# Turning a stored chunk into image order: TensorE transposes from 16 line loads, or VectorE block transposes from 4 quarter loads

## The chip, the cores and the metric

The kernel runs on one core of a Trainium2 chip. The metric is the device time of one execution in microseconds (us). The profile is one execution recorded by the hardware profiler; its span runs from its first to its last instruction.

## The reference

The input `x` is 1024 images of 16 x 16 pixels with 16 channels, in float32 (image, height h, width w, channel c). Four layers follow one another. Each normalises its input in 8 groups of 2 channels, applies an operation and adds the result to its input:

```python
x = x + _L0_conv_ref(_gn(x), core0, core1, core2)      # a tensor-train matrix over (h, w, c)
x = x + _L1_conv_ref(_gn(x), ..., 1)                   # cellular automaton, one step
x = x + _L2_conv_ref(_gn(x), filters, bias)            # 3 x 3 convolution
x = x + _L3_conv_ref(_gn(x), ..., 1)                   # cellular automaton, one step

# one step of the automaton (layers 1 and 3):
p = jnp.concatenate([xt, y1, y2], axis=1)              # the channels and two depthwise 3 x 3 filters of them
h = jax.nn.relu(p.reshape(B * W * Hh, 48) @ fc0_w.T + fc0_b)   # 128 hidden values
d = (h @ fc1_w.T + fc1_b).reshape(B, C, W, Hh)
mask = (pre & post)                                    # a pixel is alive before and after
x = (xt + d) * mask
```

The change touches none of this arithmetic. It concerns how the result of the last layer, for the first half of the images, comes from the kernel's own layout into that of the output.

## The kernel before, in words

The batch is cut into two chunks of 512 images (`NB`). Inside the layers a chunk lies with 128 pixel-and-channel lines on the partitions and its 512 images along each partition, in 32 such tiles: 64 KB in each partition, 8 MB a chunk. Two buffers of this size, `X0` and `X1`, hold a chunk each; between layers the chunks go through DRAM tensors `xf[layer][chunk]`. In `xf[4][0]`, the last layer's result for the first chunk, the shape is (8, 4, 128, 512): pairs of columns, quarters q of the channels, 128 lines (4 channels, 2 columns v of the pair, 16 heights h), 512 images. An image of the output has h, w and c along the free axis instead, so lines and images have to be exchanged.

The end of the program is what matters here. `layer_nca` (lines 1256 to 1474) is the automaton. It runs as layer 3 for chunk 0, and then for chunk 1. Per chunk it has 64 groups ("quads") of 4 output rows. For a row, TensorE makes the hidden layer in a PSUM bank `ph` by matmuls that use 32 of its 128 rows each, four of them side by side (line 1464); ScalarE applies ReLU into `hid` (line 1467). For a group, TensorE then multiplies four `hid` tiles into a bank `po` (line 1317), two groups to a bank. VectorE adds bias and input to it and frees the bank (`u`, line 1329). GpSimd applies the mask and adds the residual (lines 1366 and 1367). In the first quarter of a chunk VectorE also makes the alive flags and masks (lines 1325, 1347, 1361, 1362), from counts `pcnt` of TensorE (line 1356). The order of the slots is written out by `plan()`.

For chunk 0 a finished tile is stored to `xf[4][0]` (line 1369). For chunk 1 it stays on chip: `turn` inside `layer_nca` (line 1376) transposes it by four matmuls with an identity into a bank `ptx`, and two copies (`evac`, line 159, on VectorE in this part) put it into `xo`, which takes the room of `X0`. At the very end eight DMAs of 1 MB (line 1606) store chunk 1.

`output_steps(0)` (lines 951 to 984) is the work that is woven into chunk 1's automaton: for each height h of chunk 0, `load` brings 256 lines from `xf[4][0]`, `turn` exchanges lines and images, and `store` writes 512 pieces of 1 KB to the output. `run(layer, us, loads, *spans)` places such background steps: a step with a cost is put at a share of the main steps in proportion to the costs before it, a bare function costs 1, a number is a pause, and `(0, f)` costs nothing and comes at the place of what follows it. The order on each engine is the order of the calls; nothing reorders it afterwards. All the DMAs of this part are issued by SP, in order: `xs` loads (line 959), stores from `xo` (line 970), the residual fetches `res` (line 1298), weights `wq` (line 1275) and neighbour lines `nx` (line 1291).

In this part the PSUM banks are 6 for `h` (`ph`, `pcnt`) and 2 for `o`, which `po`, `ptx` and `ptout` take in turn (`shared[0] = "o"`). `xs` and `xo` of `output_steps` have two buffers each.

Of the kernel before, what the change touches and what calls it, by code (L numbers as in the profile page):

```python
# [18 lines left out]
B, S, C = 1024, 16, 16  # L19
P = 128  # L20
NB = 512
# [82 lines left out]
def conv_preact_kernel(ctx: ExitStack, tc: tile.TileContext, a: dict, out: bass.AP):  # L104
    nc = tc.nc
    V, A, G, T = nc.vector, nc.scalar, nc.gpsimd, nc.tensor
# [9 lines left out]
    xf = [  # L116
        [dram.tile([8, 4, P, NB], F32, tag=f"xf{l}_{n}", name=f"xf{l}_{n}") for n in range(NCH)]
        for l in range(5)
    ]
# [16 lines left out]
    def work(shape, tag, name, dt=F32):  # L136
        p, sizes = pool["sb"]
        return p.tile(shape, dt, tag=tag, name=name, bufs=sizes[tag])
# [3 lines left out]
    def bank(shape, tag, name):  # L142
        p, sizes = pool["ps"]
        if tag == "mw":
            either[0] ^= 1
            tag = "mw"[either[0]]
        return p.tile(shape, F32, tag=tag, name=name, bufs=sizes[tag])

    def psum(shape, name):
        return bank(shape, shared[0], name)  # L150
# [3 lines left out]
    def evac(dst, src):  # L154
        flip[0] ^= 1
        if flip[0] and not on_vector[0]:
            A.copy(dst, src)
        else:
            V.tensor_copy(dst, src)


    ident = const.tile([P, P], F32, tag="ident", name="ident")
# [503 lines left out]
    def rstd(st, rows=slice(0, P)):  # L666


        def root():
            st["t"] = work([P, NB], "s", "t")  # L670
            A.activation(st["t"][rows], st["ve"][rows], AF.Sqrt)

        def newton():
            ve, t = st["ve"][rows], st["t"][rows]
            st["r"] = work([P, NB], "n", "r")
            r = st["r"][rows]
            V.reciprocal(r, t)
            V.tensor_tensor(t, r, r, ALU.mult)
            V.tensor_tensor(t, t, ve, ALU.mult)
            V.tensor_scalar(t, t, -0.5, 1.5, ALU.mult, ALU.add)  # L680
            V.tensor_tensor(r, r, t, ALU.mult)

        return [2, root, 3, (6, newton)]
# [64 lines left out]
    def alone(N, q):  # L748

        return (  # L750
            N["sums"][q] + [3, N["mean"][q], 1, N["held"][q], 1] + N["sq"][q]
            + [3, N["var"][q], 1, N["keep"][q]]
        )
# [18 lines left out]
    def scaled(N, qs):  # L772
        steps = [N["spread"][qs[0]], 2, N["held"][qs[0]], 2]
        for q in qs:
            mul = N["mul"][q]
            if q < qs[-1]:
                mul = woven(mul, (2, N["spread"][q + 1]), (3, N["held"][q + 1]))
            steps += mul
        return steps
# [27 lines left out]
    def rows_in(t, w):  # L807

        return t[w // 2].rearrange("q (c v h) b -> v (q c) h b", v=2, h=S)[w % 2]
# [141 lines left out]
    def output_steps(n):  # L951

        steps = []

        def load(h, st):
            st["x"] = work([P, 2, NB], "xs", "xs")
            st["o"] = work([P, 4, 2, P], "xo", "xo")
            for w in range(S):
                nc.sync.dma_start(  # L959
                    st["x"][16 * (w % 8) : 16 * (w % 8) + 16, w // 8], rows_in(xf[4][n], w)[:, h]  # L960
                )

        def turn(bg, st):
            pt = psum([P, 2, P], "ptout")
            for wh in range(2):
                T.transpose(pt[:, wh], st["x"][:, wh, bg * P : bg * P + P], ident)  # L966
            evac(st["o"][:, bg], pt)

        def store(h, st):
            nc.sync.dma_start(  # L970
                out[n * NB : n * NB + NB, h].rearrange("(g b) w c -> b g (w c)", g=4),
                st["o"].rearrange("p g w c -> p g (w c)"),
            )

        sts = [{} for _ in range(S)]
        steps += [lambda: load(0, sts[0]), 4]
        for h in range(S):
            if h + 1 < S:
                steps.append((0, lambda h=h: load(h + 1, sts[h + 1])))
            for bg in range(4):  # L980
                steps.append(lambda h=h, bg=bg: turn(bg, sts[h]))
            steps.append((0, lambda h=h: store(h, sts[h])))
        return steps


# [544 lines left out]
    with ExitStack() as es:  # L1530
# [3 lines left out]
        loads, stat, lines, tail = input_steps(0, tag, 0, nc.sync)  # L1534
# [12 lines left out]
        loads, stat, lines, tail = input_steps(1, tag, 2, G)  # L1547
# [15 lines left out]
        for q in range(4):  # L1563
            bg = alone(N, q - 1) if q else [0.0]
            if q == 3:
                bg = bg + rstd(nst, slice(0, 96)) + [3] + scaled(N, range(3))
# [31 lines left out]
    with ExitStack() as es:  # L1598
        stage(es, dict(nca_sb, xs=2, xo=2), nca_ps)

        xo = X0.rearrange("p n b -> p (n b)").rearrange("p (g h w c) -> p g h w c", g=4, h=S, w=S)
        run(layer_nca(X1, 1, 3, L3, xo), 280, (), (output_steps(0), 0.0, 1.0))
        for h in range(0, S, 8):
            for g in range(4):
                b0 = NB + g * P
                nc.sync.dma_start(
                    out[b0 : b0 + P, h : h + 8].rearrange("b h w c -> b (h w c)"),
                    xo[:, g, h : h + 8].rearrange("p h w c -> p (h w c)"),
                )
# [27 lines left out]
```

## Time and profile before

| what | us |
|---|---|
| median of 3 runs | 3128.32 (3127.24 to 3139.66) |
| the profiled execution's own time | 3130.22 |
| its span | 3128.5 |
| mean granted TensorE clock | 0.981 |
| TensorE matmul busy | 3025.4, 97% of the span |
| VectorE busy | 1747.8, 56% |
| ScalarE busy | 1101.7, 35% |
| GpSimd busy | 685.6, 22% |
| chunk 0's automaton in layer 3, on TensorE | 2528.7 to 2787.6 |
| chunk 1's automaton in layer 3, on TensorE | 2787.6 to 3104.7 |
| last stores, after TensorE's last instruction | 3104.7 to 3128.5 |

The three stretches at the end are read from TensorE's instructions in order of time: the first is between the last convolution matmul and the first automaton matmul of the other chunk, the second ends with the last matmul of all. In the listings, a line of the timeline gives the start in us, the duration, the engine, the line of the kernel, the operation with output and input by the program's names, the shape, and how many instructions were merged into it; what stands in brackets is how long the engine sat idle before it, and what ended that. A float32 matmul leaves two records, so a group of four shows as x8. A few per cent of the matmul records are missing from a trace, so that some counts fall short.

### The profile page before, as it was taken

The numbers are of one execution on the slowest core, as the hardware profiler recorded it, in microseconds if no ns is written. First come the engines' busy times: TensorE is split into PE (matmuls) and PEld (weight loads), VectorE is DVE, ScalarE is ACT, GpSimd is POOL, SyncE is SP. The second block draws the span as 40 slices with busy tenths as digits, with TensorE's granted clock in tenths as the row PEclk, the third lists the DMA queues.
The fourth block names the chain that finished last, engine by engine and source line by source line (L and its number), as shares of the span: only waits on it lengthen the run. The fifth ranks groups of instructions, "written<-read, shape, count | busy, mean of one in ns | idle before, by whom it ended". The sixth has DMA issues, their size and how long they took to land.

```text
span 3128.5 us, 37206 instructions
## 1 busy us (share of the span) xinstructions
PE 3025.4 (97%) x13874; PEld 1261.2 (40%) x13874; DVE 1747.8 (56%) x2330; ACT 1101.7 (35%) x1798; POOL 685.6 (22%) x738
## 2 busy tenths in 40 slices
PE   7999899999999999999999999999989999999996
PEld 5544334444444444444444433333333333333332
DVE  5264237555554555544556678558767748755222
ACT  4431341000000100000111266666665755655553
POOL 1125650200000000000000034435532224432221
PEclk8999999999999999999999999999999999999998
DMA  7644654533334333322222254454455764434445
GB/s 281 237 129 99 141 123 157 174 106 106 106 106 164 117 109 110 113 99 86 86 86 92 94 165 128 129 169 158 135 175 80 182 164 152 138 89 116 136 135 184
DMA packets 242597, 418.71 MB, mean 134 GB/s; under 512 B 38117, under 2 KB 92009, under 8 KB 239345
## 3 DMA queue, kind: packets, MB, share of 16 engines
q1 hardware_dynamic: 216160, 362.46, 35.5%
q0 software_dynamic: 25440, 53.58, 8.4%
q8 instruction: 110, 1.80, 0.2%
q14 instruction: 71, 0.57, 0.1%
q10 hardware_dynamic: 816, 0.30, 0.0%
HBM read 238.79 MB, written 165.60 MB: 129 GB/s over the span
## 4 chain that ended last, share of the span: by engine, by line
issue 50%; PE 26%; POOL 8%; DMA 1%; DVE 1%; SPq 1%; POOLq 0%; ACT 0%; DVEq 0%
PE ph L1464 11%; PE po L1096 6%; PE po L1317 4%; POOL u L1366 4%; POOL res L1367 4%; PE po L1191 2%; POOL xf L1242 1%; PE ptout L966 1%; SPq L959 1%; PE L_conv_pe L392 0%; PE pw L1019 0%; PE ptx L1376 0%; DMA xn<-xf 0%; PE po L1200 0%; PE pcnt L1356 0%
## 5 line engine op out<-in xcount | busy, mean ns | idle before, releaser
L1096 PE MATMUL po<-xn,w 128*128 128x512 f32 x3584 | 1580.1, 597 | 4.6 <-DVE xn L910 4.6
L1096 PEld LDWEIGHTS po<-xn,w 128*128 128x128 f32 x3584 | 671.3, 190 | 843.4 <-issue 820.7
L1467 ACT ACTIVATE hid<-ph,pack 128x512 f32<-128x512 f32 x1024 | 654.0, 686 | 430.0 <-PE ph L1464 311.5
L1132 DVE TENSOR_TENSOR r<-r,po 128x512 f32<-128x512 f32 x576 | 378.3, 685 | 592.6 <-PE po L1096 526.8
L1366 POOL TENSOR_TENSOR u<-u,mask 128x512 f32<-128x512 f32 x128 | 203.3, 1588 | 1859.4 <-DMA nx<-xn 1267.5
L1464 PE MATMUL ph<-xn,wq 32*128 32x512 f32 x3664 | 574.7, 614 | 1.7 <-DMA wq<-L_conv_wy 1.7
L1024 ACT COPY w<-pw 128x512 f32<-128x512 f32 (+1 forms) x320 | 150.6, 557 | 1189.5 <-issue 1003.4
L1464 PEld LDWEIGHTS ph<-xn,wq 32*128 32x128 f32 x3664 | 229.1, 185 | 263.4 <-issue 229.6
L1464 PE MATMUL ph<-xn,pack 32*128 32x512 f32 x1288 | 302.1, 634 | 1.2 <-DVE mask L1362 0.9
L1317 PE MATMUL po<-hid,pack 128*32 128x512 f32 x2048 | 282.9, 609 | 3.7 <-ACT hid L1467 2.7
L1037 DVE TENSOR_TENSOR w<-w 128x512 f32<-128x512 f32 x320 | 210.7, 686 | 95.7 <-ACT w L1024 95.6
L639 DVE TENSOR_TENSOR xn<-xn,m 128x1024 f32<-128x1024 f32 x160 | 225.4, 1458 | 44.3 <-ACT m L654 44.2
L1367 POOL TENSOR_TENSOR res<-res,u 128x512 f32<-128x512 f32 x128 | 212.3, 1658 | 17.5 <-DMA res<-xf 5.1
L1329 DVE SCALAR_TENSOR_TENSOR u<-po,pack,xn 128x512 f32<-128x512 f32 x128 | 95.9, 750 | 158.9 <-PE po L1317 153.9
L1191 PE MATMUL po<-xn,convw 128*128 128x512 f32 x368 | 167.0, 606 | 5.1 <-ACT conv L1239 5.1
L1464 PEld LDWEIGHTS ph<-xn,pack 32*128 32x128 f32 x1288 | 115.5, 188 | 95.5 <-issue 62.1
L1132 DVE TENSOR_TENSOR xn<-xn,po 128x512 f32<-128x512 f32 x96 | 64.4, 685 | 125.9 <-PE po L1096 125.8
L1317 PEld LDWEIGHTS po<-hid,pack 128*32 128x32 f32 x2048 | 42.8, 108 | 192.6 <-issue 136.3
L606 DVE TENSOR_TENSOR sq<-sq 128x1024 f32<-128x1024 f32 x78 | 106.9, 1371 | 15.2 <-ACT sq L624 12.9
L1191 PEld LDWEIGHTS po<-xn,convw 128*128 128x128 f32 x368 | 69.1, 193 | 103.1 <-issue 93.1
L1019 PE MATMUL pw<-R,gq 32*128 32x256 f32 (+1 forms) x1280 | 91.6, 386 | 12.6 <-ACT xn L398 10.2
L404 POOL DMA_DIRECT2D L_conv_wy<-xn x160 | 89.1, 565 | 40.4 <-ACT xn L398 31.5
(164 smaller groups left out, 1811.4 us busy)
## 6 DMA issues: line engine op xcount, KB each, us to landing
xf<-r SPq DMA_DIRECT2D x112, 512.0 KB, 3.9
xn<-xf SPq DMA_DIRECT2D x96, 512.0 KB, 5.0
r<-xf SPq DMA_DIRECT2D x80, 512.0 KB, 4.5
wq<-L_conv_wy SPq DMA_DIRECT2D x192, 192.0 KB, 2.8
res<-xf SPq DMA_DIRECT2D x128, 256.0 KB, 3.0
xf<-res SPq DMA_DIRECT2D x96, 256.0 KB, 2.0
res<-xr SPq DMA_DIRECT2D x256, 64.0 KB, 2.8
xf<-conv POOLq DMA_DIRECT2D x64, 256.0 KB, 5.9
```

What stands on the lines that cost most here:

```text
L606: V.tensor_tensor(st["t"], st["t"], x, ALU.add)
L639: V.tensor_tensor(part, part, m().unsqueeze(1).broadcast_to([P, 2, NB]), op)
L1024: A.copy(w[:, k0:4, :, 32 * r : 32 * r + 32].rearrange("p k t (v o) -> p v (k t) o", v=2), pw[r],)
L1037: V.tensor_tensor(w[:, k], w[:, x], w[:, y], ALU.add if sign > 0 else ALU.subtract)
L1096: T.matmul(po, st["w", u][:, matrix, t], x, start=t == 0, stop=t == 3)
L1132: V.tensor_tensor(r[at], r[at], po, ALU.add if sign > 0 else ALU.subtract)
L1191: T.matmul(st["po", h][wh], conv["fw"][:, y], X[:, 16 * wh + h + y - 1], start=y == max(0, 1 - h), stop=y == min(2, S - h),)
L1317: T.matmul(po[32 * j : 32 * j + 32], nca["w1"][:, v], hid[j], start=v == 0, stop=v == 1)
L1366: G.tensor_tensor(u, u, st["m"][:, w2], ALU.mult)
L1367: G.tensor_tensor(r, r, u, ALU.add)
L1464: T.matmul(ph, w, x, start=k == 0, stop=k == len(tiles) - 1)
L1467: A.activation(h, ph, AF.Relu, bias=nca["bt"][:, r : r + 1])
```

## The change

`output_steps` alone is changed. Its three functions keep their names, and its list of steps is regrouped.

- **Load.** Before, 16 DMAs for each h, one per column w: 16 partitions (the channels) and 2 KB (the 512 images) in each. The lines then lie in two halves of 8 columns. After, 4 DMAs for each h, one per quarter g of the images: 32 partitions (q, c, v), and in each of them 8 pieces (the pairs of columns) of 128 images, 512 bytes. The tile `xs` has the same size: group g of 32 partitions holds quarter g of the images.
- **Turn.** Before, four steps for each h. Each has two 128 x 128 transposes on TensorE into a bank `ptout` and one copy of 128 x 256 to `xo`. After, one step of four `V.transpose` instructions on VectorE, which exchange rows and columns within square blocks of 32 x 32. Each takes every fourth image (f) of a partition group, a read step of 16 bytes, and writes 128 x 256 values so that h's (w, c) come out contiguous, with a write step of 64 bytes between the two columns' channels of a pair. TensorE, PSUM and the copies have no part in it.
- **Store.** One DMA per h as before, 512 pieces of 1 KB; image 4p + f comes from partition p, where it was image 128g + p.
- **Places.** A turn is one step of cost 1 where it was four. With the first load, which counts 1 too, the sum of costs falls from 65 to 17.

```diff
+        lines = xf[4][n].rearrange("w q (c v h) b -> h (q c v) w b", v=2, h=S)
+
         def load(h, st):
-            st["x"] = work([P, 2, NB], "xs", "xs")
-            st["o"] = work([P, 4, 2, P], "xo", "xo")
-            for w in range(S):
-                nc.sync.dma_start(
-                    st["x"][16 * (w % 8) : 16 * (w % 8) + 16, w // 8], rows_in(xf[4][n], w)[:, h]
-                )
-
-        def turn(bg, st):
-            pt = psum([P, 2, P], "ptout")
-            for wh in range(2):
-                T.transpose(pt[:, wh], st["x"][:, wh, bg * P : bg * P + P], ident)
-            evac(st["o"][:, bg], pt)
+            st["x"] = work([P, 8, P], "xs", "xs")
+            for g in range(4):
+                nc.sync.dma_start(st["x"][32 * g : 32 * g + 32], lines[h][:, :, P * g : P * g + P])
+
+        def turn(h, st):
+            st["o"] = work([P, 4, S, S], "xo", "xo")
+            x = st["x"].rearrange("p w (j f) -> p f w j", f=4)
+            for f in range(4):
+                V.transpose(
+                    st["o"][:, f].rearrange("p (w v) c -> p w c v", v=2), x[:, f]
+                )
 
         def store(h, st):
             nc.sync.dma_start(
-                out[n * NB : n * NB + NB, h].rearrange("(g b) w c -> b g (w c)", g=4),
-                st["o"].rearrange("p g w c -> p g (w c)"),
+                out[n * NB : n * NB + NB, h].rearrange("(p f) w c -> p f (w c)", f=4),
+                st["o"].rearrange("p f w c -> p f (w c)"),
             )
...
-            for bg in range(4):
-                steps.append(lambda h=h, bg=bg: turn(bg, sts[h]))
-            steps.append((0, lambda h=h: store(h, sts[h])))
+            steps += [lambda h=h: turn(h, sts[h]), (0, lambda h=h: store(h, sts[h]))]
         return steps
```

## The prediction

> **What bounds the kernel now.** I began with busy time by stretch, for the two runs of the same automaton at the end of the program: chunk 0's in the first line, without layout work, and chunk 1's in the second, with it; the third is the last stores. Columns: stretch, length, busy TensorE, weight loads, VectorE, ScalarE, GpSimd, then clock, DMA share, GB/s.
>
> ```profile
> 2528.70:2787.60 258.90, 256.58 (x1907) 91.96 (x1906) 175.92 (x157) 167.92 (x267) 107.79 (x65) 0.99 0.48 149
> 2787.60:3104.70 317.10, 296.14 (x2137) 107.80 (x2136) 104.76 (x193) 165.21 (x256) 81.06 (x66) 0.98 0.43 120
> 3104.70:3128.50 23.80, 0.00 (x0) 0.00 (x0) 1.01 (x2) 0.00 (x0) 0.00 (x0) 0.50 0.85 353
> ```
>
> The reader is to see that TensorE fills the first stretch to 99%, and in the second is idle for 21 us and still the busiest by far. VectorE has a third of the second stretch. So the end is set by TensorE's list of instructions plus its waits. The waits stand in the list of who waited for whom (total us, times, longest):
>
> ```profile
> PE ptout L966 <- DMA xs<-xf: 5.9, 2, 3.2
> PE ptout L966 <- DVE xn L159: 5.6, 7, 1.2
> PE ptx L1376 <- POOL res L1367: 2.9, 1, 2.9
> PE ptout L966 <- DVE u L1329: 1.7, 4, 0.4
> PE po L1317 <- DVE u L1329: 1.0, 2, 0.6
> ```
>
> Most stand in front of the step that is to go. Third, TensorE's instructions in order of time, for what a transposing pair costs and what it does to its neighbours:
>
> ```profile
> 3003.00 1.14 PE L1464 MATMUL ph<-xn,wq 32*128 32x512 f32 x8
> 3004.07 1.06 PE L1317 MATMUL po<-hid,pack 128*32 128x512 f32 x8
> 3005.07 2.00 PE L1464 MATMUL ph<-xn,wq 32*128 32x512 f32 x16
> 3007.00 0.44 PE L966 MATMUL ptout<-ident,xs 128*128 128x128 f32 x2
> 3007.37 1.14 PE L1464 MATMUL ph<-xn,wq 32*128 32x512 f32 x8
> ```
>
> Start to start a pair takes 0.37 us. But x8 of `ph` takes 1.07 to the next instruction and x16 takes 1.93: 8 records more cost 0.86, and each unbroken stretch pays 0.21 once. A pair between two `ph` stretches therefore costs 0.37 + 0.21. The start of the stretch:
>
> ```profile
> 2797.73 0.44 PE L966 MATMUL ptout<-ident,xs 128*128 128x128 f32 x1 [2.65 <-DMA xs<-xf]
> 2801.41 0.45 PE L966 MATMUL ptout<-ident,xs 128*128 128x128 f32 x1 [3.23 <-DMA xs<-xf]
> 2801.79 3.80 PE L1464 MATMUL ph<-xn,pack 32*128 32x512 f32 x16
> ```
>
> TensorE waits twice for the first load, and the next x16 takes 3.72 us to its successor instead of 1.93: half speed.
>
> **What the Trainium skill says.** "TensorE: Matmul & The Clock Gate", Part 1, says that an idle window of about 3.4 us drops the clock to half, until a busy one restores it. The last fence agrees: 5.9 us of waiting, then half speed. "DMA: Bandwidth & Descriptors", Specifications, asks for at least 512 bytes a piece; the new load is exactly there, and no row of this stretch shows such pieces. "SBUF — State Buffer", Specifications (TRN2), says that an access which goes to a new 16-byte line each time is slower; the new transposes read with a step of 16 bytes and write with 64. The trace hints at it: the copy of 128 x 256 into contiguous `xo` takes 0.42 us, the one into `xn` with a large step 0.60 (groups by line). Prices for VectorE's transpose are below.
>
> **The change, part by part.** The sum is against the profiled execution, 3130.2 us (span 3128.5 and 1.7 around it).
>
> *Removed from TensorE.* Through the whole list there are 64 pairs. Start to start, waits in front taken off, they sum to 24.2 us (0.38 each). 28 of them stand between two `ph` stretches and break them: 28 x 0.21 = 5.9. The others stand beside `po`, `ptx` or `pcnt`, where `ph` ends anyway: nothing. Waits ahead of them: 5.9 + 5.6 + 1.7 and 0.4 for a DMA = 13.6. After the first two waits, x16 of `ph` lost 1.8 and a following `po` 0.75 to the slow clock (1.75 instead of 1.00): 2.5. Together 46.2.
>
> Does something else wait in the place of these? The `xn` waits come from three users of two banks; with `po` and `ptx` alone each keeps its own bank in turn. In chunk 0's automaton TensorE has no such step and waits 3 us in all.
>
> *Removed from VectorE:* 64 copies x 0.422 = 27.0 us, off the path.
>
> *Added to VectorE:* 64 transposes of 128 x 256. The trace has none. From below: an SBUF `TENSOR_TENSOR` of 512 takes 0.685 at one element a cycle, so 256 elements cannot be far under 0.42. "VectorE: DVE Perf Modes", The three transpose paths, gives 311 ns for 128 x 128 in bf16, which I scale by one element per 1.04 ns to 0.44, an estimate. From above: the step costs the copy 0.18; twice that for read and write gives 0.8, and 1.0 is my end. I take 0.6: 38.4 us, 2.4 a turn, a net 11 us more on an engine that is idle for 212 in this stretch.
>
> Four in a row hold what is queued behind them: `u`, which frees a `po` bank, or the copies that free `ptx`, and through these TensorE. VectorE's instructions in order of time show the room:
>
> ```profile
> 3056.40 1.05 DVE L159 COPY xn<-ptx 128x256 f32<-128x256 f32 x2
> 3065.44 0.75 DVE L1329 SCALAR_TENSOR_TENSOR u<-po,pack,xn 128x512 f32<-128x512 f32 x1 [1.79 <-PE po L1317]
> ```
>
> From the end of the copies to the next `u` are 8.0 us, about 6.5 once two pairs and their breaks are out. In the built order the turns stand after such copies, or between `u` and the copies, whose bank isn't wanted before the next `ptx`, some 8 us on. 2.4 fits. I give back 2 us for irregular places in the first quarter, where masks and flags share VectorE. At 1.0 a turn takes 4.0 and still fits most times; some 6 us back.
>
> *Moved on SP.* 16 loads for each h took 7.9 to 9.2 us of SP's time, 0.5 each; 4 take about 2 (64 issues instead of 256). Behind them are `res`, `wq` and `nx`, all earlier now. The 1.7 us that TensorE waited for `wq` may go; not counted. The first load now needs all tiles of chunk 0, hence the landing of the last store: issued at 2792.1, 2.0 to land, loads issued by about 2796. `nx` left SP at 2800.0 before, so it isn't late. The first turn stands at 0.07 of the stretch (1 of 17 units of cost), some 20 us in, long after landing. Later loads come one period (16 us) ahead, and a store is issued a period after its turn: neither waits.
>
> *DMA pieces.* Bytes are equal; pieces per h go from 256 to 1024. The main queue's 216,160 packets took 35.5% of 16 engines' span: 82 ns each. If each of 12,288 added pieces costs this, it is 63 us of all engines, +23 points on a share of 43%; if cost goes by bytes, nothing. Either leaves room; who would wait are `wq` and `nx`, fetched two and three groups ahead. I take nothing, at most 5 us.
>
> *The tail* (last GpSimd chain, `ptx`, eight stores, 23.8 us) is as before.
>
> Sum: 46.2 - 2 = 44.2; 3130.2 - 44.2 = 3086.0. The median of the runs is 1.9 below the profiled execution: **3084**. A second way to it: chunk 0's stretch of 258.9, less the normalisation's matmuls in it (11.4 start to start), plus chunk 1's `ptx` (18.8 and some 3 of breaks) and a last chain of 4.5, is 274, against 317: 43 less.
>
> **The rivals.**
>
> *The waits aren't gained.* Without `ptout` in front, TensorE at the start of the stretch or in the masks' quarter may meet another late one: `nx`, GpSimd (two `u` buffers), or 512-byte pieces that make `wq` late. Then 24.2 + 5.9 stay, less some 5: 25 gained, 3103. For it: 13.6 + 2.5 are waits, and waits like to move. Against it: the equal stretch of chunk 0.
>
> *Slower: VectorE's transposes hold TensorE.* If one takes T, a turn stalls TensorE by 4T - 6.5 sixteen times. It eats the 46 at 4T = 9.4, T = 2.35 us; at 2.8 it is 75 - 46 = 29 more: 3157. For it: two awkward steps and no row for the operation. Against: it needs over five times the dense price.
>
> *More.* TensorE ran at half speed again around 2913 to 2917 (`po` 1.86, x8 of `ph` 2.2: 2.0 lost), after a wait for `xn`. If that goes, with `po` on `u` 1.0, `ptx` on `xn` 1.2, `wq` 1.7 and nothing given back: 52, 3076.
>
> *It does little.* ScalarE (165 us) or the planned slots set the pace: under 16 us gained. Chunk 0's stretch has the same ScalarE work at TensorE's pace; hardly.
>
> **How the numbers follow.** Forecast (3077 to 3093) 0.63; waits not gained (3093 to 3112) 0.19; more (under 3077) 0.09; little or nothing 0.05; slower 0.04. A measurement of this kernel can tell about 0.5% (16 us) from no change. Faster 0.91, same 0.05, slower 0.04. The range is 3074 to 3102: below it and above it some 0.05 and 0.13 are left.
>
> **What would show it.** Right: no `ptout`; the second stretch near 273 us with TensorE idle under 8; x24 of `ph` where x8 and x16 stood; full clock at the start of the stretch; transposes of 0.4 to 0.8 us; a load block on SP of about 2 us. Wrong: transposes above 1.2 us with `po` or `ptx` waiting for VectorE; a new wait of several us for `nx`, `wq` or GpSimd in TensorE's list; or a stretch that is shorter by much more than 44, which would mean that transposes cost more than their start-to-start time.

## The result, and the profile after

| | before | after |
|---|---|---|
| median of four runs each | 3127.78 (3124.84 to 3139.66) | 3079.36 (3076.64 to 3082.70) |
| the profiled execution's own time | 3130.22 | 3082.70 |
| its span | 3128.5 | 3081.0 |
| mean granted TensorE clock | 0.981 | 0.985 |
| chunk 1's automaton, on TensorE | 317.1 | 267.3 |
| from TensorE's last instruction to the end of the span | 23.8 | 23.4 |

The ratio of the times is 0.984, with a 95% interval of 0.981 to 0.987: the change makes the kernel 1.6% faster, 48 us by the medians, where 44 had been forecast.

Between the two profiled executions the difference is 47.5 us. The automaton of chunk 1 gives 49.7 of it. It starts 2.7 us later (2790.3 against 2787.6), and this difference is there already when chunk 0's automaton begins, so it comes from earlier parts that the change does not touch; the stores at the end give 0.4 back. So the stretch that the prediction worked on is the right one, and its own length is a steadier measure than the time of the whole program: in three executions with the same stores at the end (this one, and `after_again` and `forms` below) it was 267.35, 267.34 and 266.89 us, while the spans differed by 7 us (3081.0, 3079.1, 3073.7). The experiments are therefore read by the length of this stretch first.

Busy time by stretch in the changed kernel, with the columns of the first fence of the prediction:

```profile
2531.30:2790.30 259.00, 256.68 (x1909) 91.97 (x1908) 175.75 (x157) 168.07 (x267) 107.77 (x65) 0.99 0.48 149
2790.30:3057.60 267.30, 262.79 (x2009) 100.35 (x2008) 114.09 (x193) 164.01 (x256) 81.32 (x66) 1.00 0.52 142
3057.60:3081.00 23.40, 0.03 (x1) 0.00 (x0) 1.01 (x2) 0.00 (x0) 0.00 (x0) 0.50 0.87 359
```

Chunk 0's stretch is 259 us long as before. TensorE is idle for 4.5 us of the second instead of 21, at a full clock, and has 128 records fewer: the 64 pairs. VectorE works 9 us more than before and has far to go. Who waited for whom (total us, times, longest), TensorE's part of the list for the second stretch:

```profile
PE ptx L1377 <- POOL res L1368: 2.9, 1, 2.9
PE ptx L1377 <- DVE xn L159: 1.2, 1, 1.2
PE ph L1465 <- DVE mask L1363: 0.2, 1, 0.2
```

The three waits of `ptout` are gone, and nothing has taken their place. What is left is the chain of GpSimd at the very end (2.9) and two small ones; all three stood there before, at the same length. `po` no longer waits for `u` (1.0 before) nor `ph` for `wq` (1.7 before). TensorE in order of time, at the place where before it waited twice for the first load:

```profile
2796.69 1.07 PE L1318 MATMUL po<-hid,pack 128*32 128x512 f32 x8
2797.68 2.00 PE L1465 MATMUL ph<-xn,pack 32*128 32x512 f32 x16
2799.61 1.12 PE L1318 MATMUL po<-hid,pack 128*32 128x512 f32 x8
```

The x16 takes 1.93 us to its successor (from its start to that of the next instruction), not 3.72. And later in the stretch:

```profile
2993.82 2.86 PE L1465 MATMUL ph<-xn,wq 32*128 32x512 f32 x24
2996.61 1.07 PE L1318 MATMUL po<-hid,pack 128*32 128x512 f32 x8
2997.61 0.66 PE L1377 MATMUL ptx<-ident,res 128*128 128x128 f32 x4
2998.19 2.86 PE L1465 MATMUL ph<-xn,wq 32*128 32x512 f32 x24
```

Where x8 and x16 stood with a pair between them, x24 stands whole, 2.79 us to its successor: 1.07 + 1.93 would be 3.00, the break of 0.21 less. VectorE in order of time, around one turn:

```profile
3006.69 1.05 DVE L159 COPY xn<-ptx 128x256 f32<-128x256 f32 x2
3007.57 2.29 DVE L968 STREAM_TRANSPOSE xo<-xs 128x256 f32<-128x256 f32 x4
3014.17 0.75 DVE L1330 SCALAR_TENSOR_TENSOR u<-po,pack,xn 128x512 f32<-128x512 f32 x1 [4.31 <-PE po L1318]
```

The turn takes 2.3 us, right behind the copies, and then VectorE still waits 4.3 us for the next full `po`: here the room is 6.6 us. Over all 64, by its tile, a transpose takes 0.654 us in the median (0.619 to 0.897). SP's instructions in order of time show the other side:

```profile
2990.72 0.61 SPq L973 DMA_DIRECT2D out_dram<-xo  x1
2991.38 2.71 SPq L962 DMA_DIRECT2D xs<-xf  x4
2995.03 0.34 SPq L1276 DMA_DIRECT2D wq<-L_conv_wy  x1
```

A block of loads holds SP for 2.7 us here and for 1.8 to 3.7 us in the whole stretch; an issue takes 0.57 us in the median. From issue to landing a load now takes 4.3 us in the median where it took 1.9, in a period of 16 us.

Start to start, TensorE's whole list in this stretch, in us; a wait is taken off the instruction that it stands in front of:

| | before | after | difference |
|---|---|---|---|
| `ptout` | 24.16 | 0 | -24.2 |
| `ph` | 181.67 | 174.56 | -7.1 |
| `po` | 66.30 | 64.86 | -1.4 |
| `pcnt` | 4.63 | 4.21 | -0.4 |
| `ptx` | 19.69 | 19.40 | -0.3 |
| waits | 20.63 | 4.32 | -16.3 |
| sum | 317.08 | 267.35 | -49.7 |

### The profile page after: what moved, and what is told of

Same layout as the page of the kernel before. It is cut to its first block, busy times and chain, and to the rows that moved or that the text cites. A ratio compares the mean times of both kernels' runs of the same rounds, so it can differ in the third digit from the quotient of the medians.

```text
span 3081.0 us, 36641 instructions
## 1 busy us (share of the span) xinstructions
PE 2994.7 (97%) x13746; PEld 1257.7 (41%) x13746; DVE 1756.3 (57%) x2330; ACT 1100.8 (36%) x1798; POOL 686.7 (22%) x738
## 4 chain that ended last, share of the span: by engine, by line
issue 47%; PE 35%; POOL 4%; DMA 1%; DVE 1%; SPq 0%; POOLq 0%; DVEq 0%; ACT 0%
PE ph L1465 17%; PE po L1318 6%; PE po L1097 6%; PE po L1192 2%; POOL u L1367 1%; POOL res L1368 1%; POOL xf L1243 1%; PE L_conv_pe L392 0%; PE pw L1020 0%; PE pr L738 0%; PE ptx L1377 0%; PE pvar L726 0%; PE pmean L722 0%; PE po L1201 0%; DMA xn<-xf 0%
## 5 line engine op out<-in xcount | busy, mean ns | idle before, releaser
L1465 PE MATMUL ph<-xn,wq 32*128 32x512 f32 x3664 | 566.2, 610 | 0.0
```

What stands on the lines that cost most here:

```text
L1465: T.matmul(ph, w, x, start=k == 0, stop=k == len(tiles) - 1)
```

## The experiments

The theory is that of the prediction: TensorE's list sets the end, and the gain is the pairs, the breaks that they make in `ph`, the waits in front of them, and the slow clock after the first two waits. The rivals were that waits would come back elsewhere, that VectorE's transposes would hold TensorE, and that the loads, with fewer DMAs but smaller pieces, do more than was granted. The time of the kernel before, run beside each series, was 3129.71 (44 runs), 3130.35 (13 runs) and 3130.27 us (7 runs) in the median. A ratio is to the times of that kernel in the same series, with its 95% interval; what is read from a trace is one execution.

**The loads alone.** (`q_load_pe`) The kernel before, with the new load; the pairs stay on TensorE, and since the lines now lie by quarters, each of the 64 pairs needs two copies instead of one.

```diff
-            for w in range(S):
-                nc.sync.dma_start(st["x"][16 * (w % 8) : 16 * (w % 8) + 16, w // 8], ...)
+            for g in range(4):
+                nc.sync.dma_start(st["x"][32 * g : 32 * g + 32], lines[h][:, :, P * g : P * g + P])
...
+            for i in range(2):
+                T.transpose(pt[:, i], st["x"][:, 2 * k + i], ident)
```

> The quarter loads of the change (4 DMAs for each height) with the exchange left on TensorE: 128 transposes in 64 pairs as before, and two copies to a pair. If the gain comes from TensorE's list, all of its 24.2 us and 5.9 us of breaks are still there; only the waits can change, and the first load can't come before the last store has landed: 3120 to 3130 us. If the gain came from the relief of SP and of the loads, most of it is here: under 3105 us.

Measured: 3121.33 us, ratio 0.998 (0.997 to 0.999); the stretch 313.5. TensorE waits once for the first load, 3.7 us instead of 5.9, and no longer for `wq`; the x16 after it is still slow, 3.3 us to its successor. The load's part in the gain, as long as the pairs remain, is 3.6 us of the stretch in this execution and 8 us by the median. Up to 3064 us the trace is 6.5 us ahead of the kernel before; then the granted clock is 0.5 from 3093.3 on for 6.8 us, after a wait of only 0.4 us, and some 3 us are lost again. So the load gives about 4 to 8 us; the rest belongs to the pairs' leaving.

**The start waits alone.** (`late_first_turn`) The kernel before, with the first turn later. The pause pushes all later turns back a little too, and packs them closer.

```diff
-        steps += [lambda: load(0, sts[0]), 4]
+        steps += [lambda: load(0, sts[0]), 16]
```

> The kernel before with a longer pause between the first load and the first turn (16 in place of 4), so that TensorE gets to the first pair after its lines have landed. If the waits at the start of the stretch and the half-speed clock after them are a loss of their own, 5.9 + 2.5 us go: 3117 to 3122 us, and the trace shows full speed there. If something else is late at once: 3125 to 3129 us.

Measured: 3117.09 us, ratio 0.996 (0.995 to 0.997); the stretch 304.8, 12.3 less than before. TensorE in order of time:

```profile
2787.88 2.00 PE L1464 MATMUL ph<-xn,pack 32*128 32x512 f32 x16
```

The wait is gone and the clock is full: 1.93 us to the successor again. The expected 5.9 + 2.5 explain 8.4 of the 12.3. The rest is, in the main, that `wq` is 1.0 us less late, that the pairs wait 3.9 us for the `xn` copies instead of 5.6, that the second slow stretch (2.0, around 2913, after such a wait) does not come, and that `po` no longer waits for `u` (1.0), against a new wait of 1.0 for `nx`.

**The pairs alone, back at their places.** (`pairs_own_bank`) The changed kernel, with a pair of transposes of the identity wherever the kernel before had one. Each takes a bank in turn with `po` and `ptx`; nothing reads it, so no copy is needed.

```diff
+        def pair():
+            pt = psum([P, 2, P], "pdummy")
+            for i in range(2):
+                T.transpose(pt[:, i], ident, ident)
...
-            steps += [lambda h=h: turn(h, sts[h]), (0, lambda h=h: store(h, sts[h]))]
+            steps += [pair] * 4 + [(0, lambda h=h: turn(h, sts[h])), (0, lambda h=h: store(h, sts[h]))]
```

> The changed kernel with 64 idle pairs of transposes of the identity, at the places of the pairs of before, each into a bank of the pool that po and ptx share; nobody reads them. If a pair costs 0.38, a break 0.21, and a third user of two banks brings back waits for VectorE of 6 to 8 us: 24 + 6 + 7 on top of 3079, so 3113 to 3119 us, with waits of TensorE for u and xn in front of the pairs. If the waits came from the loads or the copies of before and not from the banks: 3107 to 3110 us.

Measured: 3120.58 us, ratio 0.997 (0.996 to 0.998), some 2 us above what was expected; the stretch 304.9, which is 37.6 more than in the changed kernel. The pairs take 23.3, `ph` 5.0 more (28 breaks of 0.18), and TensorE waits 9.0 more. The end is 3.9 us longer as well (27.3 instead of 23.4), because VectorE's last turn comes only after TensorE's last instruction here; with the 37.6 that makes up the difference of the medians, 41.2. The list of waits:

```profile
PE pdummy L981 <- DVE xn L159: 5.6, 7, 1.2
...
PE pdummy L981 <- DVE u L1335: 2.1, 5, 0.4
...
PE po L1323 <- DVE u L1335: 0.4, 1, 0.4
```

These pairs wait for no load and nobody reads them, yet they wait for the copies to `xn` exactly as `ptout` did, seven times and 5.6 us. So these waits come from the third user of two banks, not from what it carries. This kernel and `late_first_turn`, from the two sides, meet at 304.9 and 304.8, in part by chance, since the turns of `late_first_turn` stand at other places. So the 49.7 us are 23 for the pairs, 5 for the breaks, 8 for the bank waits and 1 for `wq` (together 37.6 with what is small), and 12 for the rest: 5.9 of waits for the first load, 4.5 by the slow clock, and 1.7 of small waits.

**Pairs that break no `ph` group and take no bank.** (`pairs_before_po`) The changed kernel; two pairs go into each new `po` bank ahead of its first matmul, which overwrites them.

```diff
                 st["po"] = bank([P, NB], "o", "po1")
+                for i in range(4 if xo is not None else 0):
+                    T.transpose(st["po"][:, i * P : i * P + P], ident, ident)
```

> The changed kernel with 64 idle pairs of transposes of the identity, four transposes ahead of each first matmul into a po bank and into that same bank, where they are overwritten: no break of a ph stretch, no further user of the banks. If TensorE pays just 0.38 a pair: 24 on top of 3079, 3101 to 3106 us. If transposes hide beside other TensorE work: under 3095 us. If each pair costs more than its start-to-start time wherever it stands: 3112 us or more.

Measured: 3098.11 us, ratio 0.990 (0.988 to 0.991); the stretch 285.5, 18.2 more than in the changed kernel. `ph` and the waits are as in the changed kernel (174.56 and 4.31 us): without a third user and without breaks there is only the work itself. It is 18.6 us, and the time is 3 us under what was expected, for two pairs that follow one another take 0.58 together, not 0.76.

**Pairs that break `ph` groups.** (`pairs_in_ph`) The changed kernel; a pair goes into one `ph` bank in four ahead of its first matmul, which overwrites it.

```diff
                 st["ph", m, j] = bank([P, NB], "h", "ph")
+                if xo is not None and j == 1:
+                    for i in range(2):
+                        T.transpose(st["ph", m, j][:, i * P : i * P + P], ident, ident)
```

> The changed kernel with 64 idle pairs of transposes of the identity, each ahead of the first matmul into the ph bank of one row in four, and into that bank, where they are overwritten: they stand between ph matmuls, most of them within a stretch. If a break costs 0.21 besides the 0.38 of a pair: 64 x 0.59 = 37, 3112 to 3118 us. If a break costs nothing: 3101 to 3106 us, as with the pairs ahead of po.

Measured: 3138.79 us, ratio 1.003 (1.002 to 1.005), and the expectation was missed by 21 us. The stretch is 325.8, 58.4 more: 0.91 a pair, with no more waiting (4.7 us). TensorE in order of time:

```profile
2961.47 1.99 PE L1468 MATMUL ph<-xn,wq 32*128 32x512 f32 x14
2963.39 0.44 PE L1457 MATMUL ph<-ident 128*128 128x128 f32 x2
2963.76 1.98 PE L1468 MATMUL ph<-xn,wq 32*128 32x512 f32 x10
2965.67 1.07 PE L1318 MATMUL po<-hid,pack 128*32 128x512 f32 x8
```

x14 and x10 are cut from an x24. Whole it takes 2.79 to the next instruction; in two it takes 1.92 + 1.91. The pair stands inside a group of eight records (four matmuls that run side by side), so that both stretches last as long as an x16, and the cut costs about a group of 0.86 and the 0.21. Other pairs of this kernel fall between groups or beside `po` and `ptx`, which fits a mean of 0.91 and not 0.37 + 1.04. The kernel before had none inside a group: its 24.2 + 5.9 us are 0.47 a pair.

**Many loads, small pieces.** (`sixteen_loads`) The changed kernel, with each load cut into four: 256 issues again, and the same number of 512-byte pieces.

```diff
-                nc.sync.dma_start(st["x"][32 * g : 32 * g + 32], lines[h][:, :, P * g : P * g + P])
+                for k in range(0, 8, 2):
+                    nc.sync.dma_start(
+                        st["x"][32 * g : 32 * g + 32, k : k + 2], lines[h][:, k : k + 2, P * g : P * g + P]
+                    )
```

> The changed kernel with each of its four loads cut into four by pairs of columns: 256 issues on SP again, the same 512-byte pieces, VectorE turns as changed. If SP's issue time was off the path: 3078 to 3084 us, with a few us for weights that come late. If the shorter load blocks on SP gave the 16.7 us of waits that have gone: 3090 to 3097 us.

Measured: 3089.05 us, ratio 0.988 (0.986 to 0.990), between the two cases and 1 us under the second. The stretch is 280.7, 13.3 longer than in the changed kernel. SP and TensorE in order of time, at the same moment:

```profile
2881.68 9.51 SPq L963 DMA_DIRECT2D xs<-xf  x16
2891.22 0.42 SPq L1279 DMA_DIRECT2D wq<-L_conv_wy  x1
```

```profile
2890.09 1.07 PE L1321 MATMUL po<-hid,pack 128*32 128x512 f32 x8
2894.03 0.69 PE L1468 MATMUL ph<-xn,wq 32*128 32x512 f32 x1 [2.87 <-DMA wq<-L_conv_wy]
...
2895.10 1.55 PE L1321 MATMUL po<-hid,pack 128*32 128x512 f32 x8
```

The weights `wq` are issued only when the block of loads has left SP, 9.5 us on, and TensorE stands 2.9 us for them; then `po` takes 1.55 instead of 1.07, at a granted clock of 0.5. Three such waits make 7.1 us, and `nx` is late by 1.0. `po` and `ph` lose 5.1: 1.4 at the start, where the waits for `nx` take groups of four apart, and the rest in 10.2 us at half the clock. The same 256 issues cost the kernel before only 1.7 us of waits for `wq` after the first load. A likely reason is that its pairs gave TensorE a slower pace, a cover that is gone with them; that is argued, not shown by itself, since the blocks of loads also stand at other places in the order.

**The same, with the weights fetched earlier.** (`sixteen_ahead`) `sixteen_loads`, with `wq` asked for three groups ahead instead of two.

```diff
-        AHEAD, FAR = 2, 3
+        AHEAD, FAR = 2 if xo is None else 3, 3
```

> The changed kernel with 16 loads for each height, and in this stage the weights wq fetched three groups ahead and not two. If the 16 loads cost their 9 us because a block of 8 to 9 us on SP makes wq late: TensorE's waits for wq go, 3078 to 3083 us. If many small loads cost time by themselves, on the DMA engines or by the number in flight: 3086 to 3092 us as with two groups.

Measured: 3086.69 us, ratio 0.986 (0.984 to 0.988), in the range of the second case, but between the changed kernel and `sixteen_loads`, with intervals that overlap both: by the time alone nothing is told. By the stretch it is 274.1, so half of the 13.3 us was the late `wq`: its wait falls from 7.1 to 0.4, and `po` is at 65.0 again. Of the 6.8 that stay, 1.5 are waits for `nx` at the start, 2.1 a further wait for GpSimd near the end, and 3.0 are in `ph`: 1.4 between the two waits for `nx`, and 1.7 in one x24 right after the wait for GpSimd, which takes 4.48 us to its successor instead of 2.79 at a granted clock of 0.5. GpSimd itself had waited for a `res`:

```profile
3039.06 1.26 POOL L1371 TENSOR_TENSOR res<-res,u 128x512 f32<-128x512 f32 x1 [6.74 <-DMA res<-xf]
```

SP issued this `res` at 3036.2, right behind a block of 16 loads of 9.7 us, and `nx` at 2800.8, right behind one of 9.0 us. So the other half is in the main late operands as well, `nx` and `res` in place of `wq`, and not the number of loads on the DMA engines.

**VectorE's room.** (`turn_twice` and `turn_four`) The changed kernel; each transpose is done twice, and in another kernel four times, to the same place.

```diff
-            for f in range(4):
+            for f in [f for f in range(4) for _ in range(2)]:
```

> The changed kernel with each VectorE transpose done twice, eight in a row of 0.65 us, 5.2 us a turn. If VectorE has 6.5 us of room between the copies from ptx and the next u: 3078 to 3083 us. If turns were already near to holding TensorE: 16 x 2.6 = 42 on top, up to 3121 us.

Measured: 3084.30 us, ratio 0.985 (0.984 to 0.987), 1 us above what was expected. The stretch is 276.4: turns of 5.1 us cost 9.0 in all, 5.4 of them in new waits, and nearly all of those stand in the first quarter, where VectorE also makes the masks. The rest is nearly all in `ph`, and the granted clock was 0.5 for 3.4 us after one of the waits. Elsewhere the turns hide, as the room of 6.5 us says.

> The changed kernel with each VectorE transpose done four times, sixteen in a row, 10.5 us a turn. If the room is 6.5 us: 16 x 4.0 = 64 on top, 3130 to 3150 us, with TensorE waiting for u and xn. If the banks and the queue of hidden tiles give more room than the order of VectorE's instructions shows: under 3110 us.

Measured: 3153.02 us, ratio 1.007 (1.005 to 1.009), 3 us above the upper end of what was expected. The stretch is 340.2, 73 more than in the changed kernel. VectorE in order of time:

```profile
2995.98 10.78 DVE L968 STREAM_TRANSPOSE xo<-xs 128x256 f32<-128x256 f32 x16
3006.66 0.71 DVE L1330 SCALAR_TENSOR_TENSOR u<-po,pack,xn 128x512 f32<-128x512 f32 x1
```

The `u` that frees a `po` bank starts the moment the turn is over, and TensorE waits for it (24.1 us in 11 times), for masks (14.3) and for the `xn` copies (16.1); `ph` and `po` run 19 us longer, and the granted clock was 0.92 in this stretch, where the changed kernel has 1.00. This is the slower rival's mechanism, and it does exist: with turns of 10.8 us the gain is more than used up. At 2.3 it is not reached.

**What the steps cost a transpose.** (`forms`) The changed kernel, with four forms of access in the four transposes of a turn; three of them leave images or channels of the first chunk in another order.

```diff
+            y = st["x"].rearrange("p w (f j) -> p f w j", f=4)
+            o = [st["o"][:, f].rearrange("p (w v) c -> p w c v", v=2) for f in range(4)]
+            d = [st["o"][:, f].rearrange("p (w v) c -> p w (v c)", v=2) for f in range(4)]
+            V.transpose(o[0], x[:, 0])
+            V.transpose(o[1], y[:, 1])
+            V.transpose(d[2], x[:, 2])
+            V.transpose(d[3], y[:, 3])
```

> The changed kernel with its four transposes of a turn in four forms: the step of 16 bytes on the read and 64 on the write as changed; contiguous read; contiguous write; both contiguous. Images or channels of the first chunk come out in another order in three of the forms; the work is the same in amount. If the steps make a transpose 0.65 us: 0.42 to 0.46 with both contiguous, one of the two others between. If a float32 transpose takes 0.65 whatever its steps: all four alike. The time stays within 3 us of the changed kernel's, since VectorE has room.

Measured in one run: 3075.4 us, the stretch 266.9. The groups of instructions by line (busy us, mean ns of one, idle before):

```profile
L970 DVE STREAM_TRANSPOSE xo<-xs 128x256 f32<-128x256 f32 x16 | 10.6, 663 | 0.0
...
L972 DVE STREAM_TRANSPOSE xo<-xs 128x256 f32<-128x256 f32 x16 | 9.6, 599 | 0.0
L971 DVE STREAM_TRANSPOSE xo<-xs 128x256 f32<-128x256 f32 x16 | 9.4, 589 | 0.0
...
L973 DVE STREAM_TRANSPOSE xo<-xs 128x256 f32<-128x256 f32 x16 | 6.6, 413 | 0.0
```

L973 reads and writes contiguous blocks, L972 reads with the step of 16 bytes, L971 writes with the step of 64, and L970 is the change's own form. Each step costs 0.18 by itself (0.19 on the read), and the two together 0.25. The place in the turn is not the reason: in the changed kernel, where all four have one form, the medians by place are 0.649 to 0.660.

**A shorter end.** (`half_tail`) The changed kernel, with half of chunk 1's result (columns 0 to 7) stored while the last four column pairs are still computed, and the other half at the end, in pieces of 512 bytes instead of 8 KB.

```diff
+            if q == 3 and w2 > 3:
+                for k in (2 * w2 - 8, 2 * w2 - 7):
+                    b0, h0 = NB + P * (k % 4), 8 * (k // 4)
+                    nc.sync.dma_start(
+                        out[b0 : b0 + P, h0 : h0 + 8, 0:8].rearrange("b h w c -> b h (w c)"),
+                        xo[:, k % 4, h0 : h0 + 8, 0:8].rearrange("p h w c -> p h (w c)"),
+                    )
```

> The changed kernel with the second chunk's columns 0 to 7 stored while its last columns are still computed, two DMAs after each of the last four tiles, and only columns 8 to 15 at the end; pieces of 512 bytes in both. The last stores are 23.6 us long at 353 GB/s. If 512-byte pieces go at near that rate: up to 10 us less, 3068 to 3073 us. If they go at half of it: nothing gained, 3077 to 3084 us.

Measured: 3072.83 us, ratio 0.982 (0.980 to 0.983); the stretch 267.3 as before. From its end to the end of the span are 18.2 us instead of 23.4. The last stretch of the program, with the columns of the first fence:

```profile
3052.80:3071.00 18.20, 0.04 (x1) 0.00 (x0) 1.01 (x2) 0.00 (x0) 0.00 (x0) 0.50 0.78 230
```

Half the bytes take three quarters of the time: over this stretch they move at 230 GB/s where the changed kernel moved 359, and in the middle of the stores (3056 to 3068 us here, 3062 to 3078 there) at 283 against 418. Whether the pieces or SP's issues, 1.6 us each here, set this rate is not separated. The change itself was run again beside it:

> The changed kernel itself beside the others of this series, on the same chip: 3076 to 3083 us, the stretch of the second chunk's automaton 267 us.

It took 3079.82 us, ratio 0.984 (0.981 to 0.986). So the shorter end is 7 us ahead by the medians and 5 by the trace, though the two intervals overlap a little; it is the fastest version here, and clearly ahead of the kernel before.

## Why the prediction was right

*What bounds the kernel* was read rightly, from the idle time of TensorE against the length of the stretch. Whatever was put on TensorE or in front of it (the pairs experiments) came out in the time. VectorE's work at 2.3 us a turn did not; at 5.1 us it cost 9 us, at 10.8 us 73. The stretch is 267.3 us, where some 273 had been named as the sign: it gave 49.7, and the sum 46.2 less the 2 given back.

*The pairs*, 24.2 in the sum: 24.2 in the table, 23.3 when put back.

*The breaks and the slow clock*, 5.9 + 2.5 = 8.4: the table has 9.3 in `ph`, `po`, `pcnt` and `ptx`. The breaks were 5.0 when put back, somewhat smaller than read from the fence; the second slow stretch, 2.0 by the list of rivals, went too and was not in the sum. That these two slips nearly balance, 5.0 + 2.5 + 2.0 = 9.5, is luck.

*When the clock slows* was read too simply. The prediction's idle window of about 3.4 us stands in no view of this place. Two stretches around the first wait, with the columns of the first fence:

```profile
2793.43:2796.84 3.41, 1.66 (x11) 0.16 (x8) 0.00 (x0) 1.91 (x4) 0.00 (x0) 1.00 0.42 96
2796.84:2800.25 3.41, 0.44 (x1) 0.18 (x1) 0.00 (x0) 0.00 (x0) 0.00 (x0) 0.50 0.38 75
```

Half the clock is granted from 2796.84 on, before the first wait has ended (2797.73), and TensorE had been idle for only 1.75 of the 3.41 us before. In all 14 traces the clock slows only at the steps of a fixed raster of 3.41 us, and the two lines are two such steps. From 2500 us on, 13 steps of this raster at full clock hold 1.75 us or more of idle TensorE, and the step after each of them is at half clock. With 1.0 to 1.7 us of idle time it went either way; with less it happened once in over 2,000 steps (`q_load_pe`, at 3093). So about half a window of waiting was enough here, not a whole one, and the measurement decides.

*The waits*, 13.6 in the sum, were 16.3: the mis-sized term. The forecast counted only what stood in front of `ptout`; the waits of `po` for `u` (1.0) and of `ph` for `wq` (1.7), named under "More", went as well. That the `xn` waits came from three users of two banks, argued from the code, is now shown.

*The 2 us given back* for irregular places in the first quarter were not needed: one wait of 0.2 for a mask is all, and that was there before. The place was still the right one to fear, since with turns twice as long the new waits appear there first.

*VectorE's transposes* were taken at 0.6 and took 0.654, within 0.42 to 1.0. The estimate for dense access, 0.44 from the Trainium skill's "VectorE: DVE Perf Modes" (The three transpose paths), lies near the 0.413 of the contiguous form, so scaling that price by elements held here. The 1.04 ns an element fits the trace of the kernel before: `TENSOR_TENSOR` takes 1.220 us for 1024 elements and 0.686 for 512, in the median. The upper bound added the copy's 0.18 for read and for write; each alone is 0.18 indeed, which agrees with "SBUF — State Buffer", Specifications (TRN2), as to the direction for the 16-byte read step, but they don't add up.

*SP* was the weak step, though it did no harm. "About 2 us" for a block is somewhat low (1.8 to 3.7), and the 1.7 us for `wq`, "not counted", went. More important, SP was judged by the kernel before, where 8 to 9 us a block were nearly hidden. `sixteen_loads` shows that at the new pace the old number of issues would have cost 13 us, above a quarter of the gain. The two parts of the change support each other: the loads alone give 4 to 8, and the turn on VectorE with 256 issues gives 36 of the 50.

*DMA pieces* cost nothing that can be found: landing takes 4.3 us instead of 1.9, well within the period, and no wait on `xs` is left. The main queue's packets rose by 9,216: by the 12,288 pieces of the prediction, less 3,072 packets of under 512 bytes, 16 for each of the 192 issues saved. The share of the DMA engines times the length of the stretch is 136 us before (0.43 x 317.1) and 139 after (0.52 x 267.3), so that of the two cases of the prediction, 63 us more or nothing, the second is near.

*The tail* stayed: 23.8 us before, 23.4 after.

The second way, from chunk 0's stretch, gave 274 for the new stretch and was 7 high. The term that was off is the 3 us of breaks: `ph`, `po` and `pcnt` take 243.6 us in chunk 1 after the change, and 248.5 in chunk 0 before, so that 5 were to be taken off and none to be added. Of the rivals, "More" came nearest with its 52 in the stretch, and the truth lies between it and the forecast.

What stays open is the clock after short waits. Around 2913 in the kernel before, half the clock follows a wait of 1.2 us for `xn` that lies within one step of the raster; `q_load_pe` has it at the same place, while other waits of this kind leave the clock full, and neither `late_first_turn` nor the changed kernel has it. The slow clock of `q_load_pe` at 3093 comes after 0.4 us of waiting.

## What to carry to other kernels

Work on a full in-order engine is priced by what its neighbours do without it: the time from start to start, the break that it makes in work that runs side by side (0.2 us between groups here, about 1 inside one), the waits of a further user of a few shared buffers, and the clock that those waits cost. When the bounding engine becomes faster, everything that was just hidden behind it has to be costed anew at the new pace, above all the issue time of a queue that also brings the next operands of that engine and of those that feed it. And where a local change is measured, the length of its own stretch tells more than the time of the whole program.

## What was not expected of the hardware

- A block transpose of 128 x 256 float32 on VectorE takes 0.413 us with contiguous access, 0.59 to 0.60 with one stepped side, and 0.66 with both.
- Two 128 x 128 float32 transposes take 0.37 us from start to start between other matmuls, but four in a row take only 0.58.
- A cut inside a group of four side-by-side matmuls cost 1.04 us where a break between groups cost 0.21.
- The clock slows only at the steps of a raster of 3.41 us, and a step with 1.75 us or more of idle TensorE was followed by half the clock in 13 of 13 cases; with 1.0 to 1.7 us it went either way. A wait of 2.1 us (`sixteen_ahead`) cost 1.7 us more in this way.
- Stores of 4 MB in 512-byte pieces ran slower than 8 MB in pieces of 8 KB: 283 against 418 GB/s in the middle, 230 against 359 with start and end.
